# A graph layer on one core: the edge stage in an order written by hand, the outer tiles' degrees moved behind the table, and another last block

## The chip, the cores and the metric

The kernel runs on one core of a Trainium2 chip. The metric is device time in microseconds of one execution, as the median of three runs. The core's engines each work through their own queue in order: TensorE (PE, whose weight loads are listed apart as PEld), VectorE (DVE), ScalarE (ACT), GpSimd (POOL), and SyncE (SP), which here only issues DMAs. They wait for one another by semaphores.

## The reference, cut to what matters

One layer of a graph network over 625 nodes of width 512 and 20,625 edges (10,000 drawn pairs in both directions and one loop for each node), sorted by target, each with one of four relations and a weight:

```python
h = relu(layernorm(x))
for r in range(4):
    w_r = where(edge_type == r, edge_weight, 0)
    total_msg += (h[src] @ W_rel[r] + b_rel[r]) * w_r[:, None]
agg = segment_sum(total_msg, dst) / maximum(segment_sum(edge_weight, dst), 1)[:, None]
x1  = layernorm(h + h @ W_self + b_self + agg) * g1 + b1
ffn = gelu(x1 @ W_ffn1 + b_ffn1) @ W_ffn2 + b_ffn2      # 512 -> 1024 -> 512
out = x + layernorm(x1 + ffn) * g2 + b2
```

All of it is float32. `segment_sum(edge_weight, dst)` is called the degree below.

## The kernel before, in words

The nodes lie in five blocks of 128 (0 to 4), the edges in 162 tiles of 128. A tile whose edges all point into block 0 or block 4 is an *outer* tile; those in between are the inner ones. 90 of the 162 tiles are taken three at a time as 30 groups, whose middle tiles carry a combined weight.

**Table stage** (to about 84 us of the span). For each relation and block, in 20 steps of some 3.5 us, TensorE makes 128 rows of the table `h @ W_rel[r]` (`table_rows`, L408: four matmuls of 128x512 in float32, which TensorE runs as two passes, so eight instructions), VectorE takes them out of PSUM with the bias (L421), and SP stores them (L423) to the tensor `table` in DRAM. Beside it the outer tiles are turned into dense matrices of node by table row, `cells`: VectorE finds, piece by piece, which edges share a cell (`line_sums`, L677 to L685), and GpSimd scatters one tile of a piece after another with an indirect DMA (`scatter`, L691). 31 tiles of block 0 and 14 of block 4 are scattered. The 18 outer tiles left over are banked in the edge stage with one-hot matrices (`node_hots` L586/L596, `weighted_hots` L604, `outer_sum` L618). The degrees are made in this stage as well: for 102 tiles (30 group middles, 72 others) VectorE writes one-hots of 38 columns (`degree_hots`, L784, in four chunks) and TensorE multiplies each by the weights (`degree_sums`, L801). The table is complete when its last store has landed; `after_stores` (L706) makes GpSimd wait for that.

The constants `COLUMNS_AT`, `LINE_AT`, `DEGREE_HOTS_AT` and their like say at which of the 20 steps a piece of this side work is put into the queues: `COLUMNS_AT` the pieces of `line_sums`, `DEGREE_HOTS_AT` the chunks of degree one-hots.

**Edge stage.** GpSimd gathers table rows for one tile after another with an indirect DMA (`gather`, L1200) into ten buffers `ms`, 102 gathers in all (three of them L1275). ScalarE and VectorE weight the rows and add the three tiles of a group (L1206, L1236), ScalarE splits off a high part `eh` (L1210, L1224), VectorE the rest `el` (L1214, L1228), and TensorE sums them into the nodes of a block with one-hots `oh` (`edge_sum`, L1260). A few tiles go in whole, as float32. For blocks 0 and 4 TensorE multiplies `cells` by the table instead (`chunk_sum`, L1370), the table's rows coming back over SP as `tr`. It also makes the self part (L446). A block whose sum is complete goes through the first norm (L434 to L932, the sum `z` with `rdeg`, the inverse degree), is turned on TensorE (L356), copied (L1433), and goes through the first product of the feed-forward part (`up`, L963: 32 matmuls of one block's 128 nodes, 64 instructions), the gelu (L969), the second product (`down`, L983), the second norm (L993, L996, L1003, L1008, with a root either in three rounds on ScalarE, L901 to L903, or for the last block by L943) and the store (L1034 on SP, two to fifteen rows of it by L1036 on ScalarE). Results of the second norm go through four buffers `ow`, handed round.

In the table stage the program's order sets every queue. In the edge stage it is a planner's: each piece of work is an operation with an engine, an estimated duration, predecessors, buffers that it takes and gives back, and a rank; `Plan.times` goes through estimated time and picks for each engine the ready operation of best rank; the queues hold what it picked, in that order. Of the inner blocks, 1 comes first, then 2, and 3 is last. For the last block of all the second product is split in 384 and 128 columns.

## Time and profile before

| | |
|---|---|
| median of three runs | 256.76 us (256.63 to 258.19) |
| the profiled execution | 256.33 us, its span 254.5 us |
| granted TensorE clock | 0.998 |
| busy share of the span | PE 94%, DVE 79%, POOL 66%, PEld 56%, ACT 41% |
| table matmuls end | 84.4 us |
| first gather issued, last gather issued | 88.39 us, 218.19 us |
| last block's transposes | 230.16 us |
| last store issued | 248.3 us |

The span starts with the first profiled instruction; 1.8 us of the execution lie around it. An engine's busy share is an average over stages with different limits, so the prediction reads each stage by itself: the table stage up to 84.4 us, the wait for the table, the stream of gathers, the way from the last gather to the last block's transposes, and the last block's feed-forward part.

### The profile page before, as it was taken

Reading aid. Unit: us, or ns where it says so; the run is one execution under the profiler, and the core shown is the slowest. Engines: PE = TensorE matmul, PEld = TensorE weight load, DVE = VectorE, ACT = ScalarE, POOL = GpSimd, SP = SyncE. Lnnn points to the kernel's source line nnn. Section 1 sums busy time; section 2 is a strip of 40 time slices with the busy share of each in tenths; the row PEclk is TensorE's granted clock in tenths of the full one; section 3 lists DMA queues with packets and bytes.
Section 4 is the critical chain, followed back from the end, with each engine's and each line's share of the span. In section 5 each row is a group of like instructions: output and inputs, shape, how many; then the busy total and the mean of one; then the engine's idle time right before and its main releaser. Section 6 shows DMA issues by size and latency. Waiting matters only on the chain.

```text
span 254.5 us, 3624 instructions
## 1 busy us (share of the span) xinstructions
PE 240.1 (94%) x1059; PEld 141.6 (56%) x1059; DVE 201.8 (79%) x480; ACT 104.1 (41%) x323; POOL 168.7 (66%) x227
## 2 busy tenths in 40 slices
PE   7899999999899999999998999999979999899991
PEld 6444444445344655555453448859639548648770
DVE  3897999999999897889987889998777967664150
ACT  3017400000024169942742449865655674604500
POOL 4478888488888777777777777777777777310000
PEclk9999999999999999999999999999999999999999
DMA  6999999992264299999999777677778778510101
GB/s 196 334 406 411 384 346 410 305 351 70 83 207 130 83 321 396 362 324 336 361 331 340 213 205 208 196 208 199 213 212 249 212 202 245 171 41 3 37 1 46
DMA packets 23833, 59.43 MB, mean 234 GB/s; under 512 B 4369, under 2 KB 8721, under 8 KB 22658
## 3 DMA queue, kind: packets, MB, share of 16 engines
q0 software_dynamic: 9696, 26.79, 34.9%
q1 hardware_dynamic: 13792, 30.90, 33.3%
q10 hardware_dynamic: 322, 1.48, 1.7%
q8 instruction: 9, 0.15, 0.3%
q14 instruction: 14, 0.11, 0.1%
HBM read 49.99 MB, written 9.17 MB: 232 GB/s over the span
## 4 chain that ended last, share of the span: by engine, by line
PE 31%; DMA 30%; DVE 27%; issue 5%; ACT 2%; POOL 2%; SPq 0%; POOLq 0%; DVEq 0%; ACTq 0%
DMA ms<-table,row_i 24%; PE ps L408 12%; PE ps L983 7%; DVE add L1236 4%; PE ps L963 4%; DVE tr L421 3%; PE acc L1260 3%; DMA table<-tr 3%; PE acc L1370 2%; DVE el L1214 2%; DVE same L677 2%; POOL ms L1200 2%; DMA xs<-in_x_dram 2%; DVE oc L784 2%; PE spin L1285 2%
## 5 line engine op out<-in xcount | busy, mean ns | idle before, releaser
L1200 POOL DMA_INDIRECT ms<-table,row_i x99 | 97.1, 980 | 30.6 <-issue 11.9
L408 PE MATMUL ps<-wr,hT 128*128 128x512 f32 (+2 forms) x168 | 71.0, 576 | 0.0
L691 POOL DMA_INDIRECT cells<-weight,cell x45 | 48.2, 1071 | 12.1 <-issue 6.3
L408 PEld LDWEIGHTS ps<-wr,hT 128*128 128x128 f32 x168 | 30.6, 190 | 33.5 <-issue 30.3
L1236 DVE SCALAR_TENSOR_TENSOR add<-ms,wgt_g,add 128x512 f32<-128x512 f32 x55 | 40.5, 750 | 9.2 <-DMA ms<-table,row_i 7.4
L963 PEld LDWEIGHTS ps<-x1T,w_sb 128*128 128x128 f32 x320 | 38.1, 191 | 3.5 <-issue 1.7
L963 PE MATMUL ps<-x1T,w_sb 128*128 128x128 f32 (+1 forms) x320 | 39.0, 275 | 0.0
L983 PE MATMUL ps<-w_sb,gT 128*128 128x512 f32 (+2 forms) x96 | 36.4, 522 | 0.0
L604 ACT ACTIVATE ohw<-os,w 128x128 fp32r<-128x128 f32 x36 | 11.3, 389 | 58.2 <-DVE os L586 58.0
L1206 ACT ACTIVATE add<-ms,wgt_g 128x512 f32<-128x512 f32 x30 | 20.7, 689 | 34.5 <-DMA ms<-table,row_i 25.8
L1370 PE MATMUL acc<-tr,sums_w 128*128 128x512 f32 x60 | 28.9, 593 | 0.0
L983 PEld LDWEIGHTS ps<-w_sb,gT 128*128 128x128 f32 x96 | 16.7, 190 | 13.5 <-issue 10.8
L1260 PE MATMUL acc<-eh,oh 128*128 128x512 f32 x33 | 17.5, 540 | 3.8 <-ACT eh L1210 3.6
L1260 PE MATMUL acc<-el,oh 128*128 128x512 f32 x33 | 19.4, 604 | 0.3 <-DVE el L1214 0.3
L1214 DVE TENSOR_TENSOR el<-add,eh 128x512 fp32r<-128x512 f32 x25 | 16.8, 684 | 2.7 <-ACT eh L1210 2.6
L446 PE MATMUL ps<-ws_sb,hT 128*128 128x512 f32 x40 | 18.9, 595 | 0.0
L1210 ACT CAST eh<-add 128x512 fp32r<-128x512 f32 x25 | 14.5, 583 | 7.1 <-DVE add L1236 6.0
L969 ACT ACTIVATE gT<-ps,bf 128x128 f32<-128x128 f32 x40 | 13.8, 363 | 4.7 <-PE ps L963 3.5
L1370 PEld LDWEIGHTS acc<-tr,sums_w 128*128 128x128 f32 x60 | 11.0, 190 | 7.9 <-issue 6.9
L1260 PEld LDWEIGHTS acc<-eh,oh 128*128 128x128 f32 x33 | 6.2, 189 | 11.8 <-ACT eh L1210 7.6
L421 DVE SCALAR_TENSOR_TENSOR tr<-ps,rx,brel_bc 128x512 f32<-128x512 f32 x15 | 11.1, 742 | 1.9 <-PE ps L408 1.9
L446 PEld LDWEIGHTS ps<-ws_sb,hT 128*128 128x128 f32 x40 | 7.5, 189 | 7.6 <-issue 7.2
(238 smaller groups left out, 308.6 us busy)
## 6 DMA issues: line engine op xcount, KB each, us to landing
tr<-table SPq DMA_DIRECT2D x11, 512.0 KB, 6.0
w_sb<-in_L_gnn_W_ffn_dram SPq DMA_DIRECT2D x2, 2048.0 KB, 9.9
table<-tr SPq DMA_DIRECT2D x15, 256.0 KB, 8.4
wr<-in_L_gnn_W_rel_dram SPq DMA_DIRECT2D x3, 1024.0 KB, 7.4
cells<-zeros SPq DMA_DIRECT2D x2, 1280.0 KB, 11.1
ms<-table,row_i POOLq DMA_INDIRECT x99, 3.9
rows<-in_rows_dram SPq DMA_DIRECT2D x1, 1536.0 KB
sums_w<-cells ACTq DMA_DIRECT2D x1, 1280.0 KB
```

Source lines behind the costliest of these rows:

```text
L408: nc.tensor.matmul(p_[:, :h.stop - h.start], hT[i][:, k, :], wr_sb[r][:, k, h], start=(k == 0), stop=(k == KD - 1))
L421: made_row.append(nc.vector.scalar_tensor_tensor(m[:, h], p_[:, :h.stop - h.start], rx[:, i, 1:2], brel_bc[:, r * D + h.start:r * D + h.st ...
L446: nc.tensor.matmul(p[0], hT[i][:, k, :], ws_sb[:, k, :], start=(k == 0), stop=(k == KD - 1))
L691: s = nc.gpsimd.indirect_dma_start(out=cells[i][:, :], out_offset=bass.IndirectOffsetOnAxis(ap=cell[i][:, k:k + 1], axis=0), in_=weight[i] ...
L963: nc.tensor.matmul(pu[:, :nn + first], w1_sb[:, k, f * P:(f + 1) * P], x1T_b()[:, k, :nn + first], start=(k == 0), stop=(k == KD - 1))
L983: nc.tensor.matmul(po[h][:n, :w], box["gT"][:, f, at], w2_sb[:, f, c], start=(f == 0), stop=(f == KF - 1))
L1200: nc.gpsimd.indirect_dma_start(out=ms[j], out_offset=None, in_=table[:, :], in_offset=bass.IndirectOffsetOnAxis(ap=row_i[:, j:j + 1], axis=0))
L1206: nc.scalar.activation(box["sum"], ms[j], AF.Copy, scale=wgt_g[:, (j - GROUP0) // EG, 0:1])
L1214: nc.vector.tensor_sub(box["low"], box["sum"], box["high"].bitcast(F32))
L1236: nc.vector.scalar_tensor_tensor(to, ms[j], wgt_g[:, k, q:q + 1], box["sum"], op0=ALU.mult, op1=ALU.add)
L1260: nc.tensor.matmul(acc[bs], w.bitcast(F32) if of.dtype == F32 else w, of, start=first, stop=last)
L1370: nc.tensor.matmul(acc[b,], sums_w[b][:, c, :], kept[(b, c) if (b, c) in kept else c], start=first, stop=last)
```

## The change

Seven things change together.

1. **The order.** `Plan.written` replaces `Plan.times`: the edge stage's 699 operations are emitted in the order of a list of numbers, `ORDER`. Buffers are handed out in that order, first returned, first given. The estimated durations of the operations change too; with `ORDER` set they have no effect on the queues.
2. **The outer tiles' degrees.** The table stage keeps the 30 group tiles (two chunks of 15). The other 72 get two one-hot operations of 36 tiles on VectorE behind the last table rows, in the two buffers `gT` of the gelu, 72 matmuls into one PSUM bank, a copy on ScalarE, four small transposes and three small VectorE operations that add the result to `rdeg`.
3. **The scatters.** 16 tiles of block 4 instead of 14 are scattered, 47 in all, and 16 instead of 18 are banked. `COLUMNS_AT` and its like move.
4. **The last block.** The inner order is 1, 3, 2. Block 2 has edges of its own in its rows 14 to 127 only (the other rows of these 128 belong to the block before it), so its first product and gelu run over 114 columns instead of 128; its store is 112 rows on SP and two on ScalarE.
5. **Engines.** ReLU of the norm for blocks 2 to 4, the degree copies and the scaling of `g1`, `g2` go from VectorE to ScalarE; GpSimd clears `dg`; the load of the parameter rows is split in two.
6. **SP.** The first two loads of table rows `tr` stand ahead of the load of block 4's `cells`.
7. **Roots.** The GpSimd root of the first norm goes with the last block, now 2.

```diff
-LINES = 999, 14
+LINES = 999, 16
+ORDER = [
+    401, 403, 406, 411, 25, 2, 440, 27, 4, 441, 404, 405, 407, 32, 442, 420, 443, 408, 414, 3, 26, 28, 444, 5, 445, 6,
...
-        order = self.times()
-        for o in order:
+        for o in self.written() if ORDER else self.times():
...
+    def written(self):
+        unused, done = {k: list(n) for k, n in self.tiles.items()}, set()
+        for n in ORDER:
+            o = self.ops[n]
+            assert all(a in done for a, _ in o.after)
+            for k in o.take:
+                if k in unused:
+                    o.buffers.setdefault(k, []).append(unused[k].pop(0))
+            for k, of, at in ((*g, 0)[:3] for g in o.give if not isinstance(g, str)):
+                unused[k].append(of.buffers[k][at] if isinstance(of, Plan.Op) else of)
+            done.add(o)
...
     def pre_norm(i, mean):
-        for c in (slice(0, D // 2), slice(D // 2, D)) if i == 0 else (slice(0, D),):
-            nc.vector.tensor_scalar(z[:, i, c], xs[:, i, c], mean, 0.0, op0=ALU.subtract, op1=ALU.max)
+        if i > 1:
+            nc.scalar.activation(rx[:, i, 2:3], mean, AF.Copy, scale=-1.0)
+            nc.scalar.activation(z[:, i, :], xs[:, i, :], AF.Relu, bias=rx[:, i, 2:3])
...
+    def outer_degree_hots(j0, nj, oc):
+        oc.append(buffer("gT").rearrange("p f q -> p (f q)").bitcast(BF16)[:, :nj * W].rearrange("p (j w) -> p j w", w=W))
+        degree_hots(j0, nj, oc[0])
+
+    def outer_degree_sums(j0, nj, oc):
...
+            if j == GROUPS:
+                box_dg["p"] = buffer("ps")
+                nc.tensor.matmul(box_dg["p"][:4, :], zeros[:, :4], zeros, start=True, stop=False)
+            nc.tensor.matmul(box_dg["p"][:4, at:at + hi - lo], w3[:, j, :], oc[0][:, j - j0, lo - s:hi - s],
+                             start=False, stop=j == ND - 1)
+
+    def outer_degree_copy():
+        box_dg["s"] = buffer("ow")[:4, :]
+        nc.scalar.copy(box_dg["s"], box_dg["p"][:4, :])
+
+    def outer_degree_rows():
+        box_dg["r"] = buffer("ps")
+        for i in range(len(outer_blocks)):
+            nc.tensor.transpose(box_dg["r"][:, 4 * i:4 * i + 4], box_dg["s"][:, i * P:(i + 1) * P], ident[:4, :4])
...
-                nc.tensor.matmul(pu[:, :nn + first], w1_sb[:, k, f * P:(f + 1) * P], x1T_b()[:, k, :nn + first],
+                nc.tensor.matmul(pu[:, low:nn + first], w1_sb[:, k, f * P:(f + 1) * P], x1T_b()[:, k, low:nn + first],
...
-    DG = 26
+    DG = 15
-    COLUMNS_AT, LINE_AT, DEGREE_HOTS_AT = (0, 2, 4, 8, 11, 12, 14), 10, (7, 9, 10, 11)
+    COLUMNS_AT, LINE_AT, DEGREE_HOTS_AT = (0, 2, 4, 7, 10, 12, 14), 9, (8, 9)
...
     inner = [b for b in range(NB) if b not in OUTER]
+    inner = [*inner[:1], *inner[:0:-1]]
```

Three places show what moves in the queues. In their rows the name ahead of `<-` is what is written, and the bracket holds what the instruction waits for: an engine, or a DMA queue slot (DMAHW for SP's and ScalarE's transfers, DMASW for GpSimd's).

**VectorE at the end of the table.** `m_19` is the last block of table rows. Before:

```order
L421 SCALAR_TENSOR_TENSOR m_18_935<-ps_3_81,rx_155,brel_bc_88 128x512 [waits PE_49]
L421 SCALAR_TENSOR_TENSOR m_19_947<-ps_0_78,rx_155,brel_bc_88 128x384 [waits PE_49]
L421 SCALAR_TENSOR_TENSOR m_19_947<-ps_1_79,rx_155,brel_bc_88 128x128 [waits PE_49]
L825 CAST x_cols_129<-x_edges_136 128x27 [waits DMASW1_49,DMASW2_49,DMASW0_49,DVE_49]
L827 TENSOR_SCALAR x_step_131<-x_cols_129 128x9 [waits DVE_49]
```

With the change:

```order
L476 SCALAR_TENSOR_TENSOR m_18_857<-ps_3_81,rx_157,brel_bc_88 128x512 [waits PE_49]
L476 SCALAR_TENSOR_TENSOR m_19_869<-ps_0_78,rx_157,brel_bc_88 128x384 [waits PE_49]
L476 SCALAR_TENSOR_TENSOR m_19_869<-ps_1_79,rx_157,brel_bc_88 128x128 [waits PE_49]
L839 TENSOR_TENSOR gT_0_900<-rel_189,row_w_190 128x1368 [waits DMAHW7_49,DMAHW5_49,DVE_49]
L839 TENSOR_TENSOR gT_1_901<-rel_189,row_w_190 128x1368
L641 TENSOR_TENSOR os_0_198<-key_165,node_row_149 128x256 [waits Activation_49]
L651 TENSOR_SCALAR od1_2_197<-node_row_149,key_165 128x440
```

Behind the last table rows VectorE first writes the two sets of degree one-hots, then one-hots of banked tiles; the columns `x_cols`, which the three gathers of L1275 need, now come behind these.

**TensorE where the first gathered rows are used.** `m_15` to `m_19` and `tr` are table rows of `chunk_sum`, `eh_0` is the high part of the first gathered tile. Before:

```order
L1370 MATMUL acc0_981<-tr_13_747,sums_w0_896 128x512
L1370 MATMUL acc0_981<-m_15_852,sums_w0_896 128x512
L1370 MATMUL acc0_981<-m_16_893,sums_w0_896 128x512
L1370 MATMUL acc0_981<-m_17_912,sums_w0_896 128x512
L1260 MATMUL acc3_2_1121<-eh_0_967,oh_126_1003 128x512 [waits DMAHW1_49,DMAHW6_49,PE_49,Activation_49]
L1370 MATMUL acc0_981<-m_19_947,sums_w0_896 128x512
L1260 MATMUL acc3_2_1121<-eh_1_968,oh_126_1003 128x512 [waits Activation_49]
L1370 MATMUL acc0_981<-tr_0_0_1050,sums_w0_896 128x512 [waits DMAHW7_49]
```

With the change (L1490 is `chunk_sum`, L1374 `edge_sum`, L889 the transposes of the degrees, L501 the self part):

```order
L1490 MATMUL acc0_910<-m_15_760,sums_w0_801 128x512
L1490 MATMUL acc0_910<-m_16_798,sums_w0_801 128x512
L1490 MATMUL acc0_910<-m_17_835,sums_w0_801 128x512
L1374 MATMUL acc3_2_1062<-eh_0_889,oh_0_902 128x512 [waits DVE_49,Activation_49]
L1490 MATMUL acc0_910<-m_19_869,sums_w0_801 128x512
L889 MATMUL ps_1_79<-ident_122,ow_0_896 128x4 [waits Activation_49]
L501 MATMUL ps_3_81<-ws_sb_92,T_0_152 128x512 x2
L1374 MATMUL acc3_2_1062<-eh_1_890,oh_0_902 128x512 [waits Activation_49]
L1490 MATMUL acc0_910<-tr_0_0_1011,sums_w0_801 128x512 [waits DMAHW7_49]
```

The first gathered tile stands ahead of the same table rows as before; the small transposes, which wait for the copy on ScalarE, and half a self part stand between the first and the second gathered tile.

**ScalarE and VectorE in the last block's part.** `gT` is the gelu, `rs_y2` and `rs_y3` the root of the second norm of the block before the last (2 before, 3 now), `ow` the four result buffers. ScalarE before:

```order
L902 ACTIVATE rs_y2_0_2029<-rs_y2_0_2029 128x1 [waits Activation_49]
L903 ACTIVATE rs_y2_0_2029<-rs_y2_0_2029 128x1 [waits Activation_49]
L969 ACTIVATE gT_3_2022<-ps_1_79,bf_92 128x128 [waits PE_49]
L1036 DMA out_0_dram<-ow_3_977 2x512 [waits DMAHW0_49,DVE_49]
L969 ACTIVATE gT_3_2022<-ps_3_81,bf_92 128x128 [waits PE_49]
L969 ACTIVATE gT_3_2022<-ps_2_80,bf_92 128x128 [waits PE_49]
L969 ACTIVATE gT_3_2022<-ps_0_78,bf_92 128x128 [waits PE_49]
L969 ACTIVATE gT_3_2022<-ps_1_79,bf_92 128x128 [waits PE_49]
```

ScalarE with the change:

```order
L1061 ACTIVATE gT_0_900<-ps_3_81,bf_93 128x114 [waits PE_49]
L1061 ACTIVATE gT_0_900<-ps_0_78,bf_93 128x114 [waits PE_49]
L1128 DMA out_0_dram<-ow_3_899 15x512 [waits DMAHW0_49,DVE_49]
L1061 ACTIVATE gT_0_900<-ps_2_80,bf_93 128x114 [waits PE_49]
L993 ACTIVATE rs_y3_0_1999<-rs_y3_0_1999 128x1
L994 ACTIVATE rs_y3_0_1999<-rs_y3_0_1999 128x1 [waits Activation_49]
L995 ACTIVATE rs_y3_0_1999<-rs_y3_0_1999 128x1 [waits Activation_49]
```

Nine such root activations of the block before the last now stand behind the last gelu, where they stood between the gelus. VectorE before, from the last step of the block before the last to the last block's first sum (L993):

```order
L895 TENSOR_SCALAR rs_y2_0_2029<-rs_y2_0_2029 128x1 [waits DVE_49]
L1480 TENSOR_SCALAR rows_89<-rows_89 128x512
L1008 SCALAR_TENSOR_TENSOR ow_3_977<-ow_0_974,rs_y2_0_2029,xs_87 128x512 [waits Activation_49]
L993 TENSOR_TENSOR ow_2_976<-ps_3_81,z_149 128x384 [waits PE_49]
L996 BN_STATS st_y3_0_2100<-ow_2_976 128x6 [waits DVE_49]
```

VectorE with the change (L1085 is the sum):

```order
L1100 SCALAR_TENSOR_TENSOR ow_3_899<-ow_0_896,rs_y1_0_1896,xs_87 128x512 [waits DVE_49,Activation_49]
L1605 TENSOR_SCALAR rows_89<-rows_89 128x512
L1100 SCALAR_TENSOR_TENSOR ow_1_897<-ow_2_898,rs_y3_0_1999,xs_87 128x512 [waits Activation_49]
L1085 TENSOR_TENSOR ow_1_897<-ps_1_79,z_151 128x384 [waits DMAHW1_49,DVE_49,PE_49]
L1088 BN_STATS st_y2_0_2067<-ow_1_897 128x6 [waits DVE_49]
```

The last block's sum goes into `ow_1`, from which the block before the last is stored just ahead of it, and waits for that store (DMAHW1); before it went into `ow_2`, which was free.

204 lines of the change are left out of this document (130 added, 74 removed), and 29 rows, old and new, of the table ORDER.

## The prediction

> **What bounds the kernel now.** I read the page first, then busy time by stage, then the timeline of each engine at the joints between stages.
>
> ```profile
> span 254.5 us, 3624 instructions
> PE 240.1 (94%) x1059; PEld 141.6 (56%) x1059; DVE 201.8 (79%) x480; ACT 104.1 (41%) x323; POOL 168.7 (66%) x227
> ```
>
> TensorE is busy 94% of the span, but that average hides which end is tight. The busy times by stage (us, window first, then its length, then PE, PEld, DVE, ACT, POOL):
>
> ```profile
> 84.40:88.40 4.00, 4.00 (x18) 2.66 (x18) 3.62 (x17) 0.39 (x2) 2.87 (x8) 1.00 0.22 67
> 88.40:219.30 130.90, 125.60 (x541) 77.73 (x539) 111.32 (x219) 78.13 (x196) 100.07 (x102) 1.00 0.83 264
> 219.30:230.20 10.90, 10.74 (x32) 5.17 (x32) 6.33 (x14) 3.43 (x13) 1.00 (x1) 1.00 0.21 65
> 230.20:238.30 8.10, 8.10 (x75) 8.04 (x74) 3.70 (x9) 4.82 (x18) 0.00 (x0) 1.00 0.09 25
> ```
>
> From the end of the table to the last block's transposes TensorE has 4.0 + 125.6 + 10.7 = 140.3 us of work in 145.8 us: 5.5 us idle. The stage is almost bound by TensorE, and is bound by something else by those 5.5 us. GpSimd's timeline says by what:
>
> ```profile
> 48.03 0.96 POOL L691 DMA_INDIRECT cells<-weight,cell  x1 [3.73 <-DVE weight L685]
> 63.78 0.96 POOL L691 DMA_INDIRECT cells<-weight,cell  x1 [0.69 <-DVE weight L685]
> 86.39 0.97 POOL L691 DMA_INDIRECT cells<-weight,cell  x1 [0.16 <-DMA table<-m]
> 88.39 1.36 POOL L1200 DMA_INDIRECT ms<-table,row_i  x1 [0.74 <-DVE od L596]
> L1200 POOL DMA_INDIRECT ms<-table,row_i x99: 942/946/1437, 88.4 to 218.2; - x99
> 218.19 1.05 POOL L1200 DMA_INDIRECT ms<-table,row_i  x1 [0.30 <-issue]
> ```
>
> The gathers take 0.95 us and start 1.25 to 1.27 us apart without a break: (218.19 - 88.39) / 101 intervals = 1.285, the three of another line included. So a chain runs through the whole stage: table complete, first gather, 102 gathers, last product, last norm, last feed-forward part. The releaser named at 88.39 is not the true one: the gather also waits for the table's stores, and they fit better:
>
> ```profile
> 70.38 14.02 PE L408 MATMUL ps<-wr,hT 128*128 128x512 f32 x40
> 84.44 0.35 DVE L421 SCALAR_TENSOR_TENSOR m<-ps,rx,brel_bc 128x128 f32<-128x128 f32 x1 [0.27 <-PE ps L408]
> ```
>
> TensorE ends the table at 84.4, the last rows leave PSUM at 84.8, and the first gather starts 4.0 us after the matmuls' end. GpSimd itself comes free at about 87.5 (86.39 + 0.97 and a small clear behind it): the two are only 0.9 us apart, so both have to come earlier.
>
> **The change part by part.** Sums are made against the profiled execution, 256.33 us; the median of the runs is 0.43 above it.
>
> *A. The first gather.* What the table stage loses:
>
> ```profile
> 46.25 0.38 PE L799 MATMUL add<-zeros 128*4 128x512 bf16 x1
> 46.47 0.81 PE L801 MATMUL add<-oc,w 128*4 128x21 bf16 x26
> 54.11 1.18 DVE L784 TENSOR_TENSOR oc<-rel,row_w 128x988 bf16<-128x988 bf16 x1
> 54.54 1.58 POOL L691 DMA_INDIRECT cells<-weight,cell  x1 [0.17 <-issue]
> 57.96 1.10 DVE L784 TENSOR_TENSOR oc<-rel,row_w 128x912 bf16<-128x912 bf16 x1
> 58.97 0.97 POOL L691 DMA_INDIRECT cells<-weight,cell  x1 [0.17 <-issue]
> ```
>
> 72 degree matmuls at 0.81 / 26 = 0.031 are 2.2 us, one clearing matmul less is 0.4: the table's matmuls end at 84.4 - 2.6 = 81.8 to 81.9, its stores at 85.9. On GpSimd the piece of cells that it waited 3.73 us for at 48.03 is put in one step earlier, with no chunk of one-hots ahead of it; I take 2.0 us of the 3.73. Two more scatters cost 2 x 1.27 = 2.5 and start from pieces that are ready some 1 to 2 us earlier, since fewer matmuls and hots stand between; the 0.69 at 63.78 should go too. Followed piece by piece, GpSimd comes free between 85.3 and 86.9. First gather at 86.6: **-1.8**. Bounds: -2.4 (the stores alone decide) and 0 (47 scatters reach as far as the 45 did).
>
> GpSimd may be slowed by the moved one-hots. The scatter at 54.54 ran beside a one-hot operation and took 1.58 instead of 0.96; the one at 58.97 began beside another and took 0.97. One of two such neighbours, then, cost 0.6. The new operations (1368 elements, 1.18 x 1368 / 988 = 1.63 each) run at about 82.3 to 85.6, beside the last scatters: at worst two times 0.6, the first gather 1.2 later and the time 255.7 as a median, a rival to which I give one chance in ten, inside the forecast's upper part. The Trainium skill ("SBUF — State Buffer", section "SBUF: two separate sides") has VectorE and GpSimd share a port pair as an exclusive lock, which a VectorE operation with two SBUF inputs takes against a GpSimd one that reads SBUF. By that rule every such neighbour would be held back; one row agrees and one does not.
>
> *B, C. From the last gather to the last block's transposes.*
>
> ```profile
> ms<-table,row_i POOLq DMA_INDIRECT x4, 3.8
> 223.30 1.88 PE L1260 MATMUL acc<-ms,oh 128*128 128x512 f32 x4
> 225.01 5.31 PE L983 MATMUL ps<-w_sb,gT 128*128 128x512 f32 x12
> 225.22 0.75 DVE L434 SCALAR_TENSOR_TENSOR z<-acc,rdeg,z 128x512 f32<-128x512 f32 x1 [1.73 <-PE acc L1260]
> 228.23 0.88 DVE L932 SCALAR_TENSOR_TENSOR z<-ow,rs_z,rows 128x256 f32<-128x256 f32 x2 [0.47 <-POOL rs_z L349]
> 230.16 0.60 PE L356 MATMUL ps<-ident,z 128*128 128x128 f32 x4
> 230.60 0.71 PE L1285 MATMUL spin<-zeros 128*128 128x256 bf16 x5
> ```
>
> The last gather is issued at 218.19 and lands 3.8 us later; its product, whole, ends only at 225.18, because TensorE did two second-product matmuls first. 6.98 us now; at the least 3.8 + 0.75 (VectorE's sum) + 0.86 = 5.4. In the new order no other work stands among the last products, but nine of them are bunched there; I take the middle, **-0.7** (0 to -1.5). From the last product to the transposes it is now 5.0 us: the norm's rows are written by 229.1, but TensorE is in its own queue through six second-product matmuls (12 instructions, 5.31). In the new order four stand there (3.5) and five spins (0.7): 4.1, just above the norm's 3.9. **-0.9** (-1.1 to 0).
>
> *D. 114 columns.*
>
> ```profile
> 69.69 0.83 PE L814 MATMUL ps<-counts,all_ones 128*128 128x3 f32 x6
> 231.15 7.31 PE L963 MATMUL ps<-x1T,w_sb 128*128 128x128 f32 x64
> 238.29 7.11 PE L983 MATMUL ps<-w_sb,gT 128*128 128x384 f32 x32
> ```
>
> If time went with columns, this would bring (238.29 - 231.15) x 14 / 128 = 0.78. But six float32 matmuls of three columns and fewer take 70.38 - 69.69 = 0.69 us, 0.115 each, and the first product's take 7.14 / 64 = 0.112 with 128 columns. Each of them loads its own 128x128 weights, and PEld is busy 8.04 of 8.10 us in that stage. So the load sets the pace and the columns do not: **-0.1** (0 to -0.78). The Trainium skill ("TensorE: Matmul & The Clock Gate", section "LDWEIGHTS (loading the stationary operand)") gives a load as columns / 1.2 ns, 107 ns for 128, whatever streams past; its section "Back-to-back issue gap" gives a lone matmul by its columns. By the first rule D is about 0, by the second -0.78, and the row of three columns sides with the first.
>
> *E. A wait at the very end.*
>
> ```profile
> 233.15 0.20 ACT L901 ACTIVATE rs_y<-rs_y 128x1 f32<-128x1 f32 x1 [0.54 <-DVE rs_y L895]
> 233.91 0.35 ACT L969 ACTIVATE gT<-ps,bf 128x128 f32<-128x128 f32 x1
> 238.50 0.37 ACT L969 ACTIVATE gT<-ps,bf 128x128 f32<-128x128 f32 x1 [0.48 <-PE ps L963]
> 243.66 0.56 DVE L993 TENSOR_TENSOR ow<-ps,z 128x384 f32<-128x384 f32 x1 [6.86 <-PE ps L983]
> 245.44 0.29 DVE L993 TENSOR_TENSOR ow<-ps,z 128x128 f32<-128x128 f32 x1 [0.63 <-PE ps L983]
> out_dram<-ow SPq DMA_DIRECT2D x2, 224.0 KB, 2.3
> out_dram<-ow SPq DMA_DIRECT2D x1, 160.0 KB, 4.2
> ```
>
> In the times of before: the last gelu ends at 238.87, three root rounds now stand behind it (some 0.85 each: one lies between 233.15 and the gelu at 233.91, which it overlaps a little), so block 3's last operation runs from 241.5 to 242.2; its store is issued and lands 2.3 (quiet) to 4.2 us later, at 244.6 to 246.5. Only then may the last block's first sum start, which TensorE has ready at 243.66; behind it in VectorE's queue is everything to the end. The second part, before at 245.44, comes at 245.7 to 247.7: **+0.5** (0.3 to 2.2).
>
> *F. Idle time.* B and C hold only if TensorE keeps up.
>
> ```profile
> 92.88 1.25 PE L618 MATMUL ps<-od,ohw 128*128 128x240 f32 x4 [0.56 <-ACT ohw L604]
> L1260 PE MATMUL acc<-eh,oh 128*128 128x512 f32 x33 | 17.5, 540 | 3.8 <-ACT eh L1210 3.6
> ```
>
> Its work from the table's end to the transposes grows by 2.2 + 0.4 (degrees), 0.3 (four transposes), 0.7 (spins) and shrinks by some 0.6 (two banked tiles) and 0.4 (one whole tile for one pair): 142.7 us, from 81.9 to 224.6 without a gap. The gathers put the transposes at 230.16 - 1.8 - 0.7 - 0.9 = 226.8, which leaves 2.2 us of idle time free; before it was 5.5, of which 3.6 waited for high parts `eh`. I take 3.0, so **+0.8** (0 to 3.3, as before).
>
> Moved work at no cost: the degrees' result is due only when the first block's sum is scaled with `rdeg`, behind most of that block's gathers; late, it would hold the accumulators and so TensorE, one microsecond for each. Their copy on ScalarE stands behind the first `eh`, and the transposes behind it in TensorE's queue have 0.9 us of table work ahead. ReLU on ScalarE, whose stage is light, would cost 0.75 for each block of which TensorE waits. The two `tr` loads ahead of `sums_w` on SP feed the same sums.
>
> Sum: -1.8 - 0.7 - 0.9 - 0.1 + 0.5 + 0.8 = -2.2, so 254.1 profiled and **254.5 us** as a median; its own range is 253 to 256.5.
>
> **The rivals.** *More of it:* stores alone decide A (-2.4), the last product follows its landing (-1.4), idle time 2.0. TensorE's line then ends at 226.6, 3.6 us early, with D and E near nothing: 252.8, median 252.3 to 253; with D at its bound 251.8. I put it at 252.2. For it: TensorE is saturated with table sums when the first gather lands. Against: three good ends at once.
>
> *No change:* idle time stays at 5.5, as each product still heads a queue behind `eh`. Transposes at 224.6 + 5.5 = 230.1; with E and D the end is 0.4 later than before: median 257.2. For it: the order is fixed in both kernels, and real landings differ from any plan.
>
> *Slower:* TensorE, in order, stands before `eh` products that ScalarE makes late, at twice the 3.8 us of the row above. Idle time 5.5 + 3.8 = 9.3, transposes at 233.9, the end 4.2 later: 260.5, median 261.0. It decides from 7.6 us of idle time on (1% slower). For it: ScalarE gets work from VectorE, and a queue written for estimated durations has no other work to offer when one is late. Against: ScalarE is busy 78 of 131 us there, and the fillers are kept between products.
>
> **How the numbers follow.** Forecast 0.42, more of it 0.23, no change 0.16, slower 0.19. About 1% (2.6 us) is what a measurement of this kernel can tell from no change: below 254.2 is faster, above 259.3 slower. Faster: nearly all of 0.23 and a little under half of the forecast, 0.42; slower 0.18; the rest 0.40. The range runs from 250.8 (A, B, C and D at their bounds together give less, at 1 in 20) to 260.2, into the slower case.
>
> **What would show it.** First gather at 86 to 87 (A); last gather to the end of the last product under 6.5 us (B); 4.1 us to the transposes (C); the first product still 7.0 to 7.1 us long (D; 6.4 would be wrong); VectorE's first sum of the last block released by a DMA (E); TensorE idle for 2 to 4 us between table and transposes (F). Idle time above 5, or a first gather at 88, would make the forecast wrong.

## The result and the profile after

| | before | after |
|---|---|---|
| median | 256.3 us (255.0 to 258.3, 18 runs) | 258.42 us (256.34 to 260.62, 18 runs) |
| ratio | | 1.0073, interval 1.0044 to 1.0101 |
| profiled execution, its span | 256.33 us, 254.5 us | 259.05 us, 257.3 us |

The change makes the kernel slower by 0.7%, less than the 1% that the prediction calls measurable, but with an interval that excludes no change; the forecast was 0.9% faster. Eight runs below, called *disturbed*, were taken where the kernel before itself took 308 to 309 us, TensorE idle for 46 of 300.7 us in one of them (14 of 254.5 before) and its granted clock 0.90 to 0.94; what disturbed them isn't known, and only rows that don't hang on it are used.

The joints of the chain, in us of the span. `relu_on_vector` is the first experiment, put here because it splits the difference:

| | before | after | relu_on_vector |
|---|---|---|---|
| VectorE's last operation on table rows starts | 84.44 | 86.11 | 82.14 |
| first gather | 88.39 | 92.73 | 88.77 |
| last gather | 218.19 | 224.71 | 220.14 |
| last block's transposes | 230.16 | 234.31 | 229.63 |
| last sum of the last block, second part | 245.44 | 249.60 | 244.92 |
| end of the span | 254.5 | 257.3 | 252.9 |

The loss is there by 17 us. TensorE's timeline at the second block's table rows (L408, after L463) is, before:

```profile
8.79 3.60 PE L408 MATMUL ps<-wr,hT 128*128 128x512 f32 x8
```

and after:

```profile
8.83 2.09 PE L463 MATMUL ps<-wr,T 128*128 128x512 f32 x4
13.45 3.54 PE L463 MATMUL ps<-wr,T 128*128 128x512 f32 x4 [2.52 <-ACT T L412]
```

Eight passes in one piece, which end at 12.39, became four, a wait of 2.52 us for ScalarE, and four more that took 3.54 and not the 2.09 of the first four, and end at 16.99. ScalarE's timeline after tells why it was late (L423 and L424 are the ReLU that the change moves there, L412 the copy of the transposed block out of PSUM):

```profile
11.96 0.20 ACT L423 ACTIVATE rx<-mv_x 128x1 f32<-128x1 f32 x1 [5.32 <-DVE mv_x L439]
12.20 0.72 ACT L424 ACTIVATE z<-xs,rx 128x512 f32<-128x512 f32 x1
12.83 0.57 ACT L412 COPY T<-ps 128x512 f32<-128x512 f32 x1
```

VectorE's timeline after, what the ReLU waited for:

```profile
9.10 0.41 DVE L697 CAST line_f<-line 128x474 f32<-128x474 int32 x1 [0.76 <-DMA line<-in_edge_line_dram]
...
11.75 0.18 DVE L439 BATCH_NORM_AGGREGATE mv_x<-st_x 128x2 f32<-128x6 f32 x1
```

Block 1's transposes are done at 8.99, but its copy stands in ScalarE's queue behind block 2's ReLU. That ReLU needs block 2's mean, which VectorE makes at 11.93, behind the edge line's columns, whose load came at 9.10. ScalarE is 5.32 us idle ahead of it. TensorE, then, waits for block 1's copy because block 2's statistics are late. The busy times by stage (us, window first, its length, then PE, PEld, DVE, ACT, POOL, the granted clock, the DMA share, GB/s) show the second half of the price:

```profile
8.90:13.40 4.50, 2.02 (x5) 0.42 (x4) 4.09 (x10) 1.40 (x3) 2.51 (x9) 0.98 1.04 368
13.40:16.90 3.50, 3.45 (x5) 1.48 (x6) 2.71 (x10) 0.93 (x2) 2.74 (x7) 0.54 1.09 417
```

In the 3.5 us behind the wait the clock is 0.54. The Trainium skill ("TensorE: Matmul & The Clock Gate", section "HAM oscillation — how this bites in real kernels") puts the abstract rule as no idle gaps above some 3.4 us; here 2.52 us were enough, and the measurement decides.

The other rows that answer to the prediction's, from the timeline of the kernel after: VectorE's degree comparisons (L839) beside GpSimd's last scatters, its first and last gather, the last products, and the last block.

```profile
86.49 3.08 DVE L839 TENSOR_TENSOR gT<-rel,row_w 128x1368 bf16<-128x1368 bf16 x2
86.84 2.07 POOL L746 DMA_INDIRECT cells<-weight,cell  x1 [0.17 <-issue]
89.22 1.19 POOL L746 DMA_INDIRECT cells<-weight,cell  x1 [0.17 <-issue]
91.88 0.10 POOL L761 MEMSET idle<- 128x2 bf16 x1
92.73 0.98 POOL L1313 DMA_INDIRECT ms<-table,row_i  x1 [0.76 <-DVE x_step L919]
224.71 0.94 POOL L1313 DMA_INDIRECT ms<-table,row_i  x1 [0.30 <-issue]
227.65 2.84 PE L1374 MATMUL acc<-ms,oh 128*128 128x512 f32 x6
234.31 0.61 PE L406 MATMUL ps<-ident,z 128*128 128x128 f32 x4
235.30 7.30 PE L1055 MATMUL ps<-T,w_sb 128*128 128x114 f32 x64
242.44 7.12 PE L1075 MATMUL ps<-w_sb,gT 128*128 128x384 f32 x32
248.47 0.56 DVE L1085 TENSOR_TENSOR ow<-ps,z 128x384 f32<-128x384 f32 x1 [2.17 <-DMA out_dram<-ow]
249.60 0.29 DVE L1085 TENSOR_TENSOR ow<-ps,z 128x128 f32<-128x128 f32 x1
```

### The profile page after: what moved, and what is told of

It reads as the page before. It is cut to its first block, busy times and chain, and to the rows that moved or that the text cites. A ratio compares the mean times of both kernels' runs of the same rounds, so it can differ in the third digit from the quotient of the medians.

```text
span 257.3 us, 3583 instructions
## 1 busy us (share of the span) xinstructions
PE 240.7 (94%) x1049; PEld 141.7 (55%) x1049; DVE 198.6 (77%) x471; ACT 107.1 (42%) x328; POOL 171.3 (67%) x232
## 4 chain that ended last, share of the span: by engine, by line
PE 52%; DVE 17%; DMA 15%; issue 5%; POOL 4%; ACT 4%; SPq 1%; DVEq 0%; POOLq 0%; ACTq 0%
PE ps L463 24%; DMA ms<-table,row_i 12%; PE acc L1490 7%; PE ps L1055 6%; PE acc L1374 5%; PE ps L501 4%; POOL ms L1313 4%; PE ps L1075 3%; DVE add L1349 3%; DMA line<-in_edge_line_dram 2%; DVE z L489 2%; DVE gT L839 1%; DVE oh L1366 1%; DVE el L1327 1%; PE ps L406 1%
## 5 line engine op out<-in xcount | busy, mean ns | idle before, releaser
L1313 POOL DMA_INDIRECT ms<-table,row_i x99 | 98.5, 994 | 31.5 <-issue 14.0
L463 PE MATMUL ps<-wr,T 128*128 128x512 f32 (+2 forms) x168 | 72.8, 587 | 2.5 <-ACT T L412 2.5
L463 PEld LDWEIGHTS ps<-wr,T 128*128 128x128 f32 x168 | 31.3, 195 | 37.5 <-issue 30.7
L1055 PEld LDWEIGHTS ps<-T,w_sb 128*128 128x128 f32 x320 | 39.0, 191 | 5.8 <-issue 2.4
L1055 PE MATMUL ps<-T,w_sb 128*128 128x128 f32 (+2 forms) x320 | 39.7, 275 | 1.4 <-ACT gT L1061 1.1
L1490 PE MATMUL acc<-tr,sums_w 128*128 128x512 f32 x60 | 29.5, 597 | 0.0
L1374 PE MATMUL acc<-eh,oh 128*128 128x512 f32 x34 | 17.5, 530 | 5.1 <-ACT eh L1323 2.0
L501 PE MATMUL ps<-ws_sb,T 128*128 128x512 f32 x40 | 18.8, 597 | 0.0
L659 ACT ACTIVATE ohw<-os,w 128x128 fp32r<-128x128 f32 x32 | 10.2, 389 | 19.4 <-DVE os L641 19.4
L1061 ACT ACTIVATE gT<-ps,bf 128x128 f32<-128x128 f32 (+1 forms) x40 | 13.9, 360 | 10.1 <-PE ps L1055 9.8
L1374 PE MATMUL acc<-el,oh 128*128 128x512 f32 x34 | 17.1, 512 | 0.0
L1490 PEld LDWEIGHTS acc<-tr,sums_w 128*128 128x128 f32 x60 | 10.8, 189 | 8.3 <-issue 7.4
L1337 ACT ACTIVATE eh<-ms,ed 128x512 fp32r<-128x512 f32 x9 | 6.3, 712 | 21.0 <-issue 16.7
L1374 PEld LDWEIGHTS acc<-eh,oh 128*128 128x128 f32 x34 | 6.4, 189 | 12.6 <-ACT eh L1337 4.2
```

The costliest lines, as they stand in the source:

```text
L463: nc.tensor.matmul(p_[:, :h.stop - h.start], hT[i][:, k, :], wr_sb[r][:, k, h], start=(k == 0), stop=(k == KD - 1))
L501: nc.tensor.matmul(p[0], hT[i][:, k, :], ws_sb[:, k, :], start=(k == 0), stop=(k == KD - 1))
L1055: nc.tensor.matmul(pu[:, low:nn + first], w1_sb[:, k, f * P:(f + 1) * P], x1T_b()[:, k, low:nn + first], start=(k == 0), stop=(k == KD - 1))
L1313: nc.gpsimd.indirect_dma_start(out=ms[j], out_offset=None, in_=table[:, :], in_offset=bass.IndirectOffsetOnAxis(ap=row_i[:, j:j + 1], axis=0))
L1374: nc.tensor.matmul(acc[bs], w.bitcast(F32) if of.dtype == F32 else w, of, start=first, stop=last)
L1490: nc.tensor.matmul(acc[b,], sums_w[b][:, c, :], kept[(b, c) if (b, c) in kept else c], start=first, stop=last)
```

## The experiments

**1. ReLU back on VectorE** (`relu_on_vector`):

```diff
     def pre_norm(i, mean):
-        if i > 1:
+        if i >= NB:
```

> The changed kernel with the ReLU of blocks 2 to 4 back on VectorE; all else as changed. Theory: the copy of block 1's transposes no longer stands behind block 2's ReLU on ScalarE, so the 2.5 us wait of TensorE at 10.9 us goes, and with it the slow clock behind it (four passes in 3.5 us instead of 2.1): the table ends about 4 us earlier, at 82, the time falls by 4 from 258.4 to 254.4, ratio to the kernel before about 0.992. Rival: the written order costs the time, in the edge stage; then the wait at 10.9 goes but the ratio stays above 1.005. Rival 2: GpSimd, with 47 scatters, holds the first gather whatever the table does: first gather stays above 91.

254.16 us, ratio to before 0.9925 (0.9893 to 0.9957). TensorE's timeline of this kernel:

```profile
9.23 3.68 PE L463 MATMUL ps<-wr,T 128*128 128x512 f32 x8
71.52 10.58 PE L463 MATMUL ps<-wr,T 128*128 128x512 f32 x32
```

The eight passes are in one piece again, the table's matmuls end at 82.1, near where the prediction's term A had them (81.8 to 81.9), and with this one condition the rest of the change is 0.75% faster than the kernel before (less than 1% too, with an interval that excludes no change), and by the two ratios some 1.5% (3.8 us) faster than the change as it was written. The theory held, and both rivals fell: the first gather came at 88.77.

**2. ReLU on ScalarE in the kernel before** (`before_relu_on_scalar`), nothing else:

```diff
     def pre_norm(i, mean):
-        for c in (slice(0, D // 2), slice(D // 2, D)) if i == 0 else (slice(0, D),):
...
+        if i > 1:
+            nc.scalar.activation(rx[:, i, 2:3], mean, AF.Copy, scale=-1.0)
+            nc.scalar.activation(z[:, i, :], xs[:, i, :], AF.Relu, bias=rx[:, i, 2:3])
```

> The kernel before with one thing of the change: ReLU of blocks 2 to 4 on ScalarE, in the same place of the program. Theory: TensorE waits some 2.5 us before block 1's table rows and runs slowly behind it; table end at about 88, ratio to before 1.014 to 1.017 (4 us). Rival: VectorE, relieved of three operations, gives it back: ratio 1.00 to 1.005.

260.41 us, ratio 1.0181 (1.0155 to 1.0207). Its timeline of ScalarE and TensorE (L412 the table's matmuls there), and its busy times behind the wait:

```profile
11.57 0.20 ACT L372 ACTIVATE rx<-mv_x 128x1 f32<-128x1 f32 x1 [5.52 <-DVE mv_x L388]
13.05 2.45 PE L412 MATMUL ps<-wr,hT 128*128 128x512 f32 x4 [2.12 <-ACT hT L362]
```

```profile
13.00:16.50 3.50, 3.44 (x9) 2.09 (x10) 3.02 (x10) 1.03 (x4) 2.62 (x7) 0.71 1.11 421
```

The wait comes without the rest of the change, and costs 1.8% there, where 1.4 to 1.7 were expected: a wait of 2.12 us was followed by 3.5 us at a clock of 0.71, and the table's matmuls end 4.4 us later than before (88.8 and 84.4).

**3. Block 2's ReLU behind the copy** (`relu_behind_copy`): it stays on ScalarE, and only the place in the queue changes:

```diff
-            nc.scalar.activation(rx[:, i, 2:3], mean, AF.Copy, scale=-1.0)
-            nc.scalar.activation(z[:, i, :], xs[:, i, :], AF.Relu, bias=rx[:, i, 2:3])
+            def relu():
+                nc.scalar.activation(rx[:, i, 2:3], mean, AF.Copy, scale=-1.0)
+                nc.scalar.activation(z[:, i, :], xs[:, i, :], AF.Relu, bias=rx[:, i, 2:3])
+            if i == 2:
+                put_off.append(relu)
+            else:
+                relu()
...
+                while put_off:
+                    put_off.pop()()
```

> The changed kernel, ReLU on ScalarE, but block 2's two activations are issued behind the copy of block 1's transposes. Theory: it is the place in ScalarE's queue and not ScalarE's ReLU as such: the wait at 10.9 goes; block 2's transposes then wait some 0.8 us for its ReLU, which ends at 12.9 against 12.0 before; the time lies 3 to 3.5 below the changed kernel, ratio to before about 0.995. Rival (ReLU on ScalarE is slower in itself, 0.72 against 0.49, and its sum of delays is what costs): ratio stays near 1.007.

255.41 us, ratio 0.9974 (0.9951 to 0.9997). ScalarE and TensorE in its timeline:

```profile
8.70 0.59 ACT L412 COPY T<-ps 128x512 f32<-128x512 f32 x1 [2.13 <-PE ps L406]
13.35 0.66 PE L406 MATMUL ps<-ident,z 128*128 128x128 f32 x4 [0.33 <-ACT z L427]
```

The copy runs at 8.70 and the 2.5 us wait is gone; the next block's transposes wait 0.33 for the ReLU itself. By the ratios this is 1.0% below the change, of 1.5% that leaving ScalarE alone brings: the place in the queue makes two thirds of the loss. The other third lies in the first steps of the table too, where ScalarE still has the ReLU: beside relu_on_vector TensorE is 0.6 us late at block 2's transposes (13.35 and 12.77), 1.1 late at block 4's (21.68 and 20.57), with a wait of 0.16 for a copy on ScalarE between them, and 1.1 late at the table's end (83.2 and 82.1). How that splits between ReLU and copies wasn't tested.

**4. The wait filled with matmuls of zeros** (`wait_kept_warm`), to part the wait from the clock:

```diff
+                if step == 0:
+                    for _ in range(12):
+                        nc.tensor.matmul(warm, zeros[:, :P], zeros, start=True, stop=True)
```

> The changed kernel with twelve matmuls of zeros (some 2.6 us) put on TensorE where it waits at 10.9 us; nothing that is computed changes. The wait itself stays. Theory: 1.4 us of the loss is the granted clock, which fell to 0.54 behind the wait; with TensorE busy it stays at 1.0 and the time falls by 1.4 against the changed kernel, ratio to before about 1.002. Rival: the four slow passes are slow for another reason (contention with loads): nothing changes, ratio 1.007.

257.12 us, ratio 1.0033 (1.0011 to 1.0056), 1.0 us below the change by the two ratios, whose intervals overlap. TensorE's timeline:

```profile
10.96 2.75 PE L1204 MATMUL warm<-zeros 128*128 128x512 bf16 x11
13.64 1.98 PE L463 MATMUL ps<-wr,T 128*128 128x512 f32 x4
```

The four passes behind the filled gap take 1.98 us instead of 3.54, the granted clock over 13.4 to 16.9 is 1.00, and the DMA share there is 1.11 as against 1.09 in the change, so contention with loads, the rival, is out. The table's matmuls end at 84.7 and not at 86.1. Of the loss some 2.5 us, then, are the wait itself, and 1.4 at the table's end (1.0 by the times) the clock behind it.

**5. Two scatters of block 4 left out** (`two_scatters_less`, run three times, the first two disturbed):

```diff
     def scatter(i, k):
+        if i == 1 and lines[1][2] - 3 <= k < lines[1][2] - 1:
+            return
```

> relu_on_vector without two of the scatters of block 4's line (the third and second last; their cells keep other contents, so block 4's sums leave those cells out). Theory (GpSimd's own queue decides when the first gather goes): the first gather comes about 2.3 to 3.3 us earlier, at 85.5 to 86.5 in place of 88.77, 0.85 behind the memset that follows the last scatter. Rival (the store of the table's last rows, or VectorE's first comparison of the first edges, decides it): GpSimd waits behind that memset, and the first gather stays above 88; with the store alone, at 86.6 to 87.5.

> The kernel of two_scatters_less once more (block 4's sums leave out the cells of two scatters): there the table itself ended so late that the store of its rows decided (a 4.80 us wait of GpSimd's memset for it), which is not so in relu_on_vector. Theory (GpSimd's queue decides the first gather there): it comes at 85.5 to 86.5 in place of 88.77. Rival (a store or VectorE decides): GpSimd waits at the memset or at the gather, and the first gather stays above 86.6; then the two scatters that the change adds would have cost less than their 2.6.

In these two the table ended late, and GpSimd's clear waited 4.80 us for its stores in the first: they told nothing of the undisturbed case.

> The kernel of two_scatters_less (block 4's sums leave out the cells of two scatters), in an execution whose clock stands as in relu_on_vector's. Theory (GpSimd's queue decides when the first gather goes): with two scatters less the first gather comes 2.3 to 3.3 us earlier, at 85.5 to 86.5 in place of 88.77. Rival (the store of the table's last rows, or VectorE, decides): GpSimd waits at its memset or at the gather, and the first gather stays above 86.6.

252.48 us (two executions only), ratio 0.9822 (0.9700 to 0.9943). GpSimd's timeline (lines are 2 higher here):

```profile
84.81 0.10 POOL L763 MEMSET idle<- 128x2 bf16 x1
85.65 1.17 POOL L1315 DMA_INDIRECT ms<-table,row_i  x1 [0.74 <-DVE os L641]
217.73 0.95 POOL L1315 DMA_INDIRECT ms<-table,row_i  x1 [0.30 <-DVE add L1351]
```

The first gather comes 3.1 us earlier than in relu_on_vector, as expected, 0.84 behind the start of GpSimd's small clear, as in all the undisturbed runs (0.84 to 0.86): 87.55 to 88.39 before, 91.88 to 92.73 after. What fills these 0.84 us isn't shown; the VectorE line that is named as releaser changes from run to run while the time does not. The table's end moved only 0.3. So GpSimd's own queue sets the first gather, and the stores, to which the prediction gave it, had at least 2.8 us of slack in relu_on_vector; 2.4 of the 3.1 us reach the last gather, 2.0 the end. A scatter, then, costs the kernel about 1 us (1.0 by the two spans, 1.3 by the ratios, with a wide interval).

**6. The degree comparisons moved away from the last scatters.** Ops 2 and 4 of the written order are the two comparisons (L839), 3 and 5 TensorE's sums of them, 6 the copy on ScalarE, 33 the second high part there, 0 and 1 the first edges' rows. Three versions of relu_on_vector; in the first the list stands in one line, and later line numbers are 31 lower.

```diff
-401, 403, 406, 411, 25, 2, 440, 27, 4, 441, ... 414, 3, 26, 28, 444, 5, 445, 6, 37, ... 33, 446, 0, ... 38, 1, 29, 50, 447, 448, ... 451, 30, 452, 7
+hots_behind_first_gathers: ... 38, 1, 2, 3, 4, 5, 6, 29, 50, 447, 448, ...
+hots_and_sums_later:       ... 38, 1, 2, 4, 29, 50, 447, 448, ... 451, 452, 3, 5, 6, 30, 7
+one_comparison_later:      ... 25, 2, 440, 27, 441, ... 414, 4, 3, 26, 28, 444, 445, 37, ... 33, 446, 5, 6, 0
```

> relu_on_vector with one thing more: the two comparisons on VectorE for the outer tiles' degrees (line 839, 1.54 us each, the pair 3.08 at 82.52), and TensorE's sums of them, stand in the written order behind the first gathers instead of beside GpSimd's last scatters. Theory (a scatter that begins during such a comparison ends only when the comparison does): the scatters that took 2.07 and 1.19 take 0.97 as the others do, GpSimd's last scatter ends 1.3 earlier, and the first gather with it, 88.8 to 87.5; the comparisons now stand beside gathers, and lengthen two of those instead (about 2.0 and 1.2 in place of 0.98), so the last gather comes at 219.5 to 220.5 (220.1 in relu_on_vector), and the time is 253.5 to 254.5 (254.16 there). Rival (the long scatters have a cause of their own, in their descriptors or their DMA queue): the two scatters keep 2.07 and 1.19 and the first gather stays at 88.8.

> The kernel of hots_behind_first_gathers once more, since TensorE's granted clock fell again and again in that execution. There a gather beside the two comparisons took 2.15 and the next 1.17, while four of the five last scatters took 0.96 to 1.03 and one 1.30: a wait of that size went with the comparisons. Expected now: the first gather at 87.5 in place of 88.8, two longer gathers behind it, the last gather at 219.5 to 220.5, and 253.5 to 254.5 us beside relu_on_vector's 254.16. Rival (GpSimd's queue doesn't decide the first gather): it stays at 88.8, and the longer gathers then make it 0.5 to 1.3 slower.

These two were disturbed, and the table ended late; the long operations did move with the comparisons (2.15 and 1.17 at the gathers in both).

> The kernel of hots_behind_first_gathers, where the clock stands as in relu_on_vector. Theory (a scatter or gather that begins during one of the two comparisons ends only with it, and GpSimd's queue decides the first gather): the last scatters take 0.97, the first gather comes at 87.5 in place of 88.77, a gather takes about 2.15 and the next 1.17 beside the comparisons; the last gather at 219.5 to 220.5 and 253.5 to 254.5 us (254.16 in relu_on_vector). Rival (the first gather isn't GpSimd's): it stays at 88.8, and the time grows by the lengthened gathers, 0.5 to 1.3.

257.58 us, ratio 1.0044 (1.0014 to 1.0073). Its timeline of GpSimd and TensorE, and its busy times behind the wait:

```profile
85.63 0.96 POOL L715 DMA_INDIRECT cells<-weight,cell  x1 [0.15 <-issue]
87.65 0.98 POOL L1282 DMA_INDIRECT ms<-table,row_i  x1 [0.64 <-DVE oh L1335]
92.74 1.72 POOL L1282 DMA_INDIRECT ms<-table,row_i  x1 [0.30 <-issue]
93.74 2.73 PE L848 MATMUL ps<-gT,w 128*4 128x21 bf16 x72 [3.69 <-issue]
```

```profile
94.00:100.00 6.00, 5.86 (x74) 3.63 (x70) 3.08 (x4) 3.38 (x8) 4.78 (x5) 0.50 1.01 386
```

The wait of GpSimd went with the comparisons, as forecast: the scatters took 0.96, a gather beside them 1.72, and the first gather came 1.1 us earlier. The time did not follow. TensorE's sums stood ahead of the table passes that used to fill this place, so it waited 3.69 us (the row names no releaser, but the sums start 0.1 us behind the end of the first comparison, at 93.64), and the next 6 us ran at a clock of 0.50. I expected to see that gone with the sums behind those passes:

> hots_behind_first_gathers with TensorE's sums of the two comparisons behind the four passes that remain for the self products, in place of ahead of them. There TensorE waited 3.69 us for the comparisons at 90.0 and then ran at a granted clock of 0.50 in the six us that followed (six passes in 4.72). Theory (that wait, and the clock behind it, ate the gain of 1.1 and 3 us more, as the 2.5 us wait in the first stage did): with work ahead of the sums the wait is below 2 us, the clock stays at 0.95 or more, and the time is 253.3 to 254.8. Rival (the lengthened gathers, or the wait of the first products, did it): 256.5 or more at a full clock.

258.90 us, ratio 1.0089 (1.0064 to 1.0113). The timeline of ScalarE and TensorE, and the busy times behind:

```profile
95.15 1.06 PE L879 MATMUL ps<-gT,w 128*4 128x38 bf16 x36 [0.38 <-DVE gT L839]
98.87 0.56 ACT L884 COPY ow<-ps 4x512 f32<-4x512 f32 x1
99.48 0.41 PE L889 MATMUL ps<-ident,ow 4*128 4x4 f32 x4 [2.84 <-ACT ow L884]
```

```profile
100.00:106.00 6.00, 6.00 (x24) 3.02 (x25) 3.31 (x13) 4.09 (x9) 4.05 (x5) 0.72 0.73 210
```

The wait for the comparisons shrank to 0.38, but the sums were late, the copy fell behind two more high parts in ScalarE's queue, and TensorE waited 2.84 us for it at its transposes; the clock behind was 0.72. The expectation missed, and this run doesn't tell what the lengthened gathers alone cost.

> relu_on_vector with the second of the two comparisons (line 839, 1.54 us) moved behind the own tiles' hots on VectorE (lines 641 and 651), still ahead of the first gather, and TensorE's sum of it (18 rows, 1.06 us) behind two more of the table's passes. Theory (a scatter that begins during a comparison ends with it, and with two in a row it can't slip in between): the last scatters take about 1.2, 1.0 and 1.0 in place of 2.07, 1.19 and 0.97, the first gather comes at 87.6 to 87.9 in place of 88.77, TensorE gets no new wait, since its sum comes where it had such work, and the time is 253.0 to 253.6 (254.16 there). Rival (GpSimd's gain is eaten behind the table, as in hots_behind_gathers_third): the first gather comes earlier, and the time stays at 254.2 or above.

258.21 us, ratio 1.0076 (1.0045 to 1.0107). Its timeline where the comparison, the copy and their neighbours stand:

```profile
82.39 1.58 DVE L839 TENSOR_TENSOR gT<-rel,row_w 128x1368 bf16<-128x1368 bf16 x1
82.75 2.06 POOL L746 DMA_INDIRECT cells<-weight,cell  x1 [0.17 <-issue]
88.41 0.98 POOL L1313 DMA_INDIRECT ms<-table,row_i  x1 [0.75 <-issue]
99.21 0.72 ACT L1337 ACTIVATE eh<-ms,ed 128x512 fp32r<-128x512 f32 x1 [4.80 <-DMA ms<-table,row_i]
99.84 0.56 ACT L884 COPY ow<-ps 4x512 f32<-4x512 f32 x1
100.45 0.59 PE L889 MATMUL ps<-ident,ow 4*128 4x4 f32 x4 [4.52 <-ACT ow L884]
```

Its busy times behind the wait:

```profile
100.00:106.00 6.00, 5.55 (x12) 2.86 (x12) 3.81 (x14) 5.70 (x14) 4.35 (x4) 0.50 0.93 337
```

Two things went wrong. The scatter at 82.75 still took 2.06: it began 0.36 us into the comparison, waited for its end at 83.97, and took 0.84 more. I had read its 2.07 as a wait for both. And the copy now stood behind the second high part, which waits for its landing until 99.21: the loss of experiment 2 again, at another place, with a 4.52 us wait of TensorE and a clock of 0.50.

**7. The last block on 128 columns** (`last_block_128_columns`): `low=ep.rows[blocks[0]][0]` becomes `low=0`.

> relu_on_vector with the last block's first product on all 128 columns again, in place of 114, and its activations likewise. Theory (the weight load sets the pace of these products): the 64 products take 7.14 us from the first start to the last end as with 114, the time is that of relu_on_vector, 254.16 within 0.4. [...]

The run was disturbed, so its time says nothing; in the last block the clock stood at 1.00, and TensorE's timeline there can be used:

```profile
285.21 7.31 PE L1055 MATMUL ps<-T,w_sb 128*128 128x128 f32 x64
292.36 7.11 PE L1075 MATMUL ps<-w_sb,gT 128*128 128x384 f32 x32
```

285.21 to 292.36 is 7.15 us, against 235.30 to 242.44 = 7.14 with 114 columns, where a price by columns would be 0.78 (the prediction's sum): the columns don't set the pace. That the weight load does is the reading that is left, with PEld busy for all 7.15 us of this stretch; no run varies the load.

**8. The last store as 112 rows in the kernel before** (`before_last_store_112_rows`; 16 rows go to ScalarE's queue). From VectorE's last result to the end of the span are 5.9 us before (248.59 to 254.5) and 4.6 after (252.74 to 257.3); I took the smaller stores for the cause.

> The kernel before with one edit: the last block's 128 rows are stored as 112 rows on SyncE's queue and 16 rows on ScalarE's, as a block of 114 rows is stored as 112 and 2. Theory (a store of 112 rows lands sooner than one of 128, since the end of the changed kernel is 4.6 us behind VectorE's last result and that of the kernel before 5.9): the end comes 0.8 to 1.3 us sooner, 255.1 to 255.7 beside 256.4. Rival (the difference is the chance of one execution, or comes with fewer bytes): no change, within 0.4.

> The kernel of before_last_store_112_rows once more. Theory (112 rows land sooner than 128): 0.8 to 1.3 us sooner than the kernel before. Rival: no change, within 0.4.

Both disturbed, the ratios too wide to tell (0.9826 to 1.0112, 0.9858 to 1.0207).

> The kernel of before_last_store_112_rows, where the clock stands. Theory (112 rows land sooner than 128): 0.8 to 1.3 us sooner than the kernel before. Rival: no change, within 0.4.

256.36 us, ratio 1.0006 (0.9971 to 1.0041), and 5.5 us (249.48 to 255.0). The theory fell. What makes the 1.3 us stays open; the kernels with block 2 last have 4.6 to 4.8.

**9. The planner's order in place of the written one** (`planners_order`: relu_on_vector with `ORDER = []`).

> relu_on_vector with the planner's order of the edge stage in place of the written one (the list ORDER empty, as it is in the kernel before). My theory gives the written order nothing: from the first gather to the last block's transposes the changed kernel took 141.58 us and the kernel before 141.77. So 254.2 within 0.7, with the last gather 131 to 132 behind the first. Rival (the written order has gained something that the two late scatters and longer gathers ate): slower by 1 to 4 us, with more idle time of TensorE behind the table.

Disturbed: ratio 1.0017 (0.9886 to 1.0149).

> relu_on_vector with the planner's order of the edge stage in place of the written one. Theory (the written order brings nothing by itself): 254.2 within 0.7. Rival: slower by 1 to 4 us, with more idle time of TensorE behind the table.

262.96 us, ratio 1.0276 (1.0226 to 1.0325). TensorE's timeline near the last gathers, and the busy times:

```profile
206.32 0.71 PE L1343 MATMUL acc<-eh,x_hots 128*128 128x512 f32 x1 [2.83 <-DVE z L458]
216.89 0.79 PE L1343 MATMUL acc<-eh,oh 128*128 128x512 f32 x1 [4.80 <-ACT eh L1292]
```

```profile
208.00:220.00 12.00, 6.69 (x15) 3.11 (x14) 9.71 (x22) 6.01 (x15) 9.26 (x10) 0.78 0.71 205
```

My expectation missed by 9 us. The planner's order of this block sequence makes TensorE wait 2.83 and 4.80 us near the end of the gathers, at a clock of 0.78; in relu_on_vector the longest wait of the stage is 1.87. From the first gather to 218.0 TensorE is idle for 10.4 us here, and for 5.9 in the gathers' stage of relu_on_vector. That the stage took 141.6 to 141.8 us in both the kernel before and the changed one was no sign that the written order brings nothing: without it the new arrangement is 3.5% slower by the two ratios. The planner works with the changed estimates of duration here, so this holds for the new arrangement alone.

## Why the prediction was wrong

**The step that failed** is in the part on moved work: "ReLU on ScalarE, whose stage is light, would cost 0.75 for each block of which TensorE waits". The price was taken from the duration of one activation and the load of the engine. What counts is what stands behind it in ScalarE's queue and when its input comes: block 1's copy stood behind block 2's ReLU, and that behind VectorE's statistics. It cost TensorE a wait of 2.5 us, and the clock behind it 1.0 to 1.4 more (experiments 1 to 4). The prediction asked for each wait's followers in the edge stage, but did not follow ScalarE's queue through the first 20 us. No rival had this mechanism; the slower one, waits for `eh`, is not what happened.

**A, the first gather.** Forecast 1.8 us earlier, measured 4.3 later. The removed degree matmuls brought nearly what was forecast (table end 82.1 with ReLU back). But the reading that the stores "fit better" than GpSimd's queue was wrong (experiment 5): the first gather stands 0.84 to 0.86 us behind GpSimd's small clear in every undisturbed run, and two more scatters with 1.3 us of waiting keep it late: 88.77 even with the table 2.3 us earlier than before, 0.4 beyond the bound at 0. Without that waiting the clear comes at 86.80 (experiment 6), inside the prediction's 85.3 to 86.9; the 0.84 behind it, which the prediction took for a wait for the stores, was missing in its sum.

**The scatters beside the comparisons**, given one chance in ten, held: 2.07 and 1.19 instead of 0.96. The row at 58.97, taken as evidence against, began 0.09 us ahead of the comparison's end at 59.06, so it had next to nothing to wait for. The kernel before had four such pairs and not two: the scatters at 42.82 and 49.30 also began during a comparison (from 42.15 and 48.33, 1.18 each) and took 1.34 and 1.04. All four end 0.84 to 0.88 us behind the comparison. They then agree with the Trainium skill ("SBUF — State Buffer", section "SBUF: two separate sides"): an exclusive lock, held for the whole instruction.

**B and C** were right in the changed kernel: from the last gather to the last product's end 5.8 us (forecast 6.3, "under 6.5"), on to the transposes 3.8 (forecast 4.1). **D** was right: 7.14. **E**: the first sum was released by the DMA, as said, but the price was 0 and not 0.5: the second part comes 7.16 us behind the start of the second product (242.44 to 249.60), before it was 7.15. Before, VectorE waited 0.63 us for TensorE there (the row at 245.44); after, the first sum starts 0.66 later behind the second product's start (6.03 and 5.37), and uses up just that wait.

**F** was too good. From the busy times by stage of the kernel after, the gathers' stage:

```profile
92.70:224.70 132.00, 125.38 (x585) 79.03 (x585) 107.41 (x217) 75.81 (x187) 100.35 (x101) 1.00 0.80 256
```

132.0 - 125.4 = 6.6 us idle where 3.0 were forecast; ahead of and behind this stage TensorE has no gap (6.8 and 9.6 us, all busy), so it has 141.8 us of work where 142.7 were forecast. Of the idle time 3.7 us wait for high parts `eh` (3.6 before), 1.3 for sums `z` (0.8 before) and 1.1 for a gelu (none before). In relu_on_vector 5.9 us are idle (131.30 less 125.44). The 102 gathers take 132.0 us after and 131.4 in relu_on_vector against 129.8, which eats what B and C bring. Here the "no change" rival, idle time stays, was right.

In sum from table to end: the table 4.0 us late, idle time 3.6 above the forecast, work 0.9 below it, and 1.7 us less behind the transposes (1.3 of it the unexplained end, 0.5 term E): 5.0 us, which is 259.05 against the forecast's 254.1. So the ReLU, 3.8 us by the ratios, is more than the whole loss against the kernel before, and the largest part of the forecast's miss; the idle time is the next. That relu_on_vector's profiled 254.65 lies near 254.1 is luck: there idle time 2.9 above the forecast, work 1.0 below it and an end 1.5 shorter nearly cancel. Both signs that the prediction named against itself, a first gather at 88 or later and idle time above 5, came in both kernels.

Three of the prediction's sums are slightly off, and none decides anything: the two terms of C, 3.5 and 0.7, give 4.2 and not 4.1; those of F give 142.9 and not 142.7; and "more of it", 252.8 as profiled, is 253.2 as a median and not 252.2.

## What to carry to other kernels

Before an operation moves to a "light" engine, write down what stands behind it in that in-order queue and when its own input comes: a busy share of 41% says nothing about either. Where TensorE waits some 2 us or more, add the clock that may fall behind the wait to its price. And where two things come free within a microsecond of each other, as the stores and GpSimd's queue here, find out by making one of them shorter before a gain is put on the other.
